# Three edits at the joints of a four-layer graph kernel: filling matmuls, the home of four sums, the order of the last three norms

## The chip, the cores and the metric

The kernel runs on one core of a Trainium2 chip. The metric is the device time of one execution in microseconds; the median of three executions is given.

## What is computed

Four layers over x (8 graphs of 2048 nodes with 64 features, float32) share one dense 2048 x 2048 adjacency matrix A. Each layer adds its result to its input and normalises over the 64 features. Cut to what matters:

```python
# layer 0: Chebyshev graph convolution with a weight per node, w[n] = embedding[n] @ weight
x = ln(x + sum_k (T_k(A) x)[n] @ w[n, k] + b[n])       # T_0 = I, T_1 = A, T_2 = 2 A A - I
# layer 1: two plain steps
z = relu(A x @ W0);  z = relu(A z @ W1);  x = ln(x + z)
# layer 2
x = ln(x + x @ W_self + (A x) @ W_neigh + b2)
# layer 3: diffusion convolution, both supports are A
x = ln(x + [x, Ax, 2AAx - x, Ax, 2AAx - x] @ W3 + b3)

def ln(x): return (x - mean(x)) / sqrt(var(x) + 1e-5)
```

Nearly all the work is products of A with a 2048 x 512 matrix (8 graphs times 64 features).

## The kernel before

x lies in SBUF as `xy`, 128 nodes by 16 node tiles by two slots by 512 columns; a pair p of graphs is 128 columns. A node group i is four node tiles (`TG` = 4). The weights are folded so that the mean over features is zero before a norm, which leaves a norm only squares, a sum, a root and a scaling.

**The first product**, A x of layer 0, goes by four slices of output nodes (L877). Slice 0 is a plain product, `plain_slice` (L767); it takes the slices' matrix chunks in the order `AHEAD` (L162), the first in four parts. Slices 1 to 3 (`fast_slice`, L791) use one level of Winograd's form of Strassen's algorithm, and VectorE meanwhile prepares sums of blocks of A (`prepare`, L622), which GpSimd's queue stores to DRAM as `comb` for the later products. A slice's result is four tiles hT of features by nodes, in the pool tag "t" (5 buffers, L761). Each is stored to DRAM as t1T on SP's queue (L754) and transposed back to nodes (`back`, L763), and so becomes the next product's input. Ahead of all this, TensorE multiplies a tile of zeros with itself eight times while the first data are on their way (L695 to L699).

**The later products** (`product`, L211) use two levels of that algorithm: 7 outer products, each an `inner` (L232) of 7 block products of 8 matmul records per 128 x 512 bank. The outer order is A11, S1, A12, S2, S4, S3, A22. An `inner` needs four sums of its right-hand blocks, t1 to t4 (L242 to L245), which VectorE writes to fresh tiles of tag "t", so they take the buffers that hT or earlier sums give back. The block products come in a fixed order, 0, 5, 1, 6, 4, 3, 7; the second takes t2, the fourth t3. Results are gathered in tiles of tag "C" (4 buffers, L230), each of four blocks: u and v from A11 and S1, and one more for each of two later places. Before the second product, tag "C" holds the block sums of `prepare`.

The order of work on an engine is partly the program's order (`keep_in_program_order`), partly a scheduler's; a pool's tile goes to whichever buffer the scheduler finds free. A `Pump` (L30) runs the layers' smaller jobs one step behind each block product.

**The last product** (`onto_slot=1`, `ends=True`, L1062) has nodes on partitions. Its last `inner` ends in `tail` (L337), which norms its last three blocks: block 3 is added by `finish(3, ...)` (L296) and normed as a job of the pump; block 2 ("1") and block 1 are joined to their partial sums, squared on ScalarE, reduced on VectorE, and so on in an order written out by hand (L355 to L375). The last block product is cut in two halves of two node tiles each (L303, L256), so block 1 has two norms, h0 and h1, of two tiles each. `Norm` (L453) holds the steps: `square`, `add_up`, `variance`, `root` (ScalarE), `refine` (one Newton step, three VectorE instructions), `scale` (VectorE) or `scale_tiles` (ScalarE, one instruction per tile and graph), `store`.

Of the kernel before, what the change touches and what calls it, by code (L numbers as in the profile page):

```python
# [9 lines left out]
F32 = mybir.dt.float32  # L10
# [93 lines left out]
def kernel(  # L104
# [106 lines left out]
    def product(src, feature, between=None, rate=1, own=None, pin=False, runs=None, onto_slot=None, ends=False):  # L211
# [10 lines left out]
        def add(out, a, b, op=ALU.add):  # L222
            nc.vector.tensor_tensor(out, a, b, op)  # L223
            return out

        def new_t():
            return sums.tile([P, NT // 2, 4 * F], F32, tag="T", name="T", bufs=3)

        def new_c():
            return sums.tile([P, 4, GW], F32, tag="C", name="C", bufs=4)  # L230

        def inner(q, b, finish, early=None, tail=None, next_sum=None):  # L232


            b11, b12, b21, b22 = (
                b[:, hm * TG : (hm + 1) * TG, ts(hc, 2 * F)] for hm in range(2) for hc in range(2)
            )

            def new():
                return sums.tile([P, TG, 2 * F], F32, tag="t", name="t", bufs=5)  # L240

            t1 = add(new(), b12, b11, ALU.subtract)  # L242
            t2 = add(new(), b22, t1, ALU.subtract)
            t3 = add(new(), b22, b12, ALU.subtract)
            t4 = add(new(), b21, t2, ALU.subtract)  # L245
            if next_sum is not None:
                next_sum()

            def mul(ps, s, xb, start, stop=True):
                a = load(q, s)  # L250
                if onto_slot is not None:

                    for k in range(TG):
                        for m in range(TG):
                            if isinstance(ps, list):
                                to, opens = ps[k // 2][:, ts(k % 2, P)], k % 2 == 0  # L256
                            else:
                                to, opens = ps[:, ts(k, P)], k == 0
                            nc.tensor.matmul(  # L259
                                to, a[:, k, m, :], xb[:, m, :], start=(start and opens and m == 0),  # L260
                                stop=(m == TG - 1), skip_group_check=True,
                            )
                    pump.step(pump.rate)
                    return
                for m in range(TG):
                    nc.tensor.matmul(  # L266
                        ps, xb[:, m, :], a[:, :, m, :], start=(start and m == 0),
                        stop=(m == TG - 1), skip_group_check=True,
                    )
# [24 lines left out]
            pc = bank("c")  # L294
            mul(pc, 4, t1, True)
            finish(3, pc, u3)  # L296
            if tail is None:
                mul(pb, 3, t4, False)
                finish(2, pb, p1)
                mul(pc, 7, b22, False)  # L300
                finish(1, pc, u2)
            else:
                halves = [p_z.tile([P, GW], F32, tag="z", name=f"mmd{h}") for h in range(2)]  # L303
                tail(pc, pb, halves, lambda: mul(pb, 3, t4, False), lambda: mul(halves, 7, b22, True))
# [29 lines left out]
        def at_the_end(c, ih, ch):  # L334


            def tail(pc, pb, halves, mul2, mul1):  # L337
                pin = tc.keep_in_program_order
                add(c[:, 1], pc, c[:, 1])
                mul2()  # L340
                i = 2 * ih
                n2 = Norm(tiles_of(i + 1), 2 * ch, 1, onto_slot, "1")
                pin(nc.vector.tensor_tensor(n2.flat(), tiled(pb), tiled(c[:, 2]), ALU.add))
                n2.square()
                mul1()
                h = [Norm(slice(i * TG + 2 * k, i * TG + 2 * k + 2), 2 * ch + 1, 1, onto_slot, f"h{k}") for k in range(2)]

                def join(k):
                    half = halves[k][:, : 2 * P].rearrange("p (t c) -> p t c", t=2)
                    pin(nc.vector.tensor_tensor(  # L350
                        h[k].flat(), half, tiled(c[:, 1])[:, 2 * k : 2 * k + 2], ALU.add
                    ))
                    h[k].square()

                n2.add_up()  # L355
                join(0)
                n2.variance()
                n2.root()
                h[0].add_up()
                n2.refine()  # L360
                join(1)
                h[0].variance()
                h[0].root()
                n2.scale_tiles(0, 2)
                h[1].add_up()
                h[1].variance()
                h[0].refine()
                h[1].root()
                n2.scale_tiles(2, 4)
                n2.store(nc.scalar)  # L370
                h[1].refine()
                h[1].scale()
                h[1].store()
                h[0].scale()
                h[0].store()  # L375
            return tail

        def tiled(block):
            return block.rearrange("p (t c) -> p t c", t=TG)
# [7 lines left out]
        def prior(ih, ch):  # L387
# [6 lines left out]

        pump.pass_mark()
        u, v = new_c(), new_c()
        t1 = new_t()
        inner(A11, b11, *fresh(u), next_sum=lambda: tc.keep_in_program_order(
            nc.vector.tensor_tensor(t1, b12, b11, ALU.subtract)
        ))  # L400
        if pump.hold:
# [48 lines left out]
    def tiles_of(i):  # L450
        return slice(i * TG, (i + 1) * TG)

    class Norm:  # L453
# [3 lines left out]
        def __init__(self, tiles, p0, n, slot, tag, pin=True):  # L457
            self.tiles, self.p0, self.n, self.slot, self.tag = tiles, p0, n, slot, tag
            self.pin = tc.keep_in_program_order if pin else lambda inst: inst
            self.nt = tiles.stop - tiles.start  # L460
            self.shape = [P, self.nt, 2 * n, F]
            self.v = self.flat().rearrange("p t (b f) -> p t b f", f=F)

        def flat(self):
# [13 lines left out]
        def square(self, pool=False):  # L478
            if self.n == 1:
                self.sq = sums.tile([P, TG, 2, F], F32, tag="t", name="sq1", bufs=5)[:, : self.nt]  # L480
            else:
                self.sq = small.tile([P, TG, 4, F], F32, tag="sq", name="sq")
            if pool:

                nc.gpsimd.tensor_tensor(self.sq, self.v, self.v, ALU.mult)
            else:
                self.pin(nc.scalar.activation(self.sq, self.v, AF.Square))

        def add_up(self):
            self.ss = self.new("ss")  # L490

            tc.keep_in_program_order(nc.vector.tensor_reduce(self.ss, self.sq, AX.X, ALU.add))

        def variance(self):
            self.pin(nc.vector.tensor_scalar(self.ss, self.ss, 1.0 / F, EPS, ALU.mult, ALU.add))
# [10 lines left out]
            self.pin(nc.vector.scalar_tensor_tensor(nw, nw, -0.5, self.ss, ALU.mult, ALU.mult))  # L506
            self.pin(nc.vector.scalar_tensor_tensor(self.rs, nw, 1.5, self.rs, ALU.add, ALU.mult))

        def scale(self):
            self.pin(nc.vector.tensor_tensor(self.v, self.v, self.wide(self.rs), ALU.mult))  # L510

        def scale_tiles(self, t0, t1):
            for t in range(t0, t1):
# [5 lines left out]
        def store(self, queue=nc.sync):  # L519
            for k in range(self.n):  # L520
                p = self.p0 + k
                queue.dma_start(out[:, p, self.tiles], xy[:, self.tiles, self.slot, ts(p, 2 * F)])

    def layernorm(i, p0, n, slot, mean=False, store=False, pool_sq=False):

# [35 lines left out]
    if True:  # L561
# [127 lines left out]
        with tc.tile_pool(name="p_n", bufs=4, space=PSUM) as p_n, tc.tile_pool(  # L689
# [5 lines left out]
            zero = sums.tile([P, GW], F32, tag="p1", name="zero")[:, :P]  # L695
            nc.vector.memset(zero, 0.0)
            rise = p_tn.tile([P, TG, P], F32, tag="pt", name="rise")
            for k in range(8):
                nc.tensor.matmul(rise[:, k % TG, :], zero, zero, start=True, stop=True)  # L699

            bias0 = small.tile([P, F], F32, tag="bias0", name="bias0")
# [409 lines left out]
```

## Time and profile before

| | |
|---|---|
| runs, not profiled | 1672.47, 1672.82, 1674.05 us (median 1672.82) |
| the profiled execution's own time | 1675.26 us |
| its span, first to last instruction | 1673.5 us |
| TensorE busy | 1661.9 us (99%) |
| VectorE busy | 946.2 us (57%) |
| ScalarE, GpSimd busy | 266.4 us (16%), 246.0 us (15%) |
| mean DMA rate | 234 GB/s |

PE is TensorE's matmuls, PEld its weight loads, DVE VectorE, ACT ScalarE, POOL GpSimd, SP SyncE, which here only issues DMAs. An fp32 matmul shows as two records. In a timeline the columns are the start and the duration in us, the engine with the line, the operation with output <- input, the shapes and the count of merged records; in brackets stands the idle time ahead of it and what ended it. In the list of waits the columns are who waited for whom, the total in us, how often, and the longest. An engine name with a q is its queue, on which it issues DMAs.

### The profile page before, as it was taken

How to read it: one execution, taken by the hardware profiler on the slowest of the kernel's cores; microseconds unless marked ns; L12 is line 12 of the kernel's file. 1: busy time of each engine (PE TensorE's matmuls, PEld its weight loads, DVE VectorE, ACT ScalarE, POOL GpSimd, SP SyncE). 2: the span in 40 equal slices, each digit the busy share in tenths (PEclk: the TensorE clock that was granted, in tenths of full speed). 3: DMA queues.
4: the chain of work that ended last, by engine and by line, in shares of the span. 5: the costliest groups of instructions: out<-in, count | busy, mean ns of one | idle time of the engine just before them, and what ended most of it. 6: DMA issues, size and time to landing. Idle time of an engine off the chain costs nothing.

```text
span 1673.5 us, 20693 instructions
## 1 busy us (share of the span) xinstructions
PE 1661.9 (99%) x8176; PEld 1046.0 (63%) x8176; DVE 946.2 (57%) x1699; ACT 266.4 (16%) x773; POOL 246.0 (15%) x332
## 2 busy tenths in 40 slices
PE   9999999999999999999999999999999999999997
PEld 4688844444444444444454455599998455579997
DVE  5487884456456456654434365873568344453667
ACT  0000000143143044430010011220001011100002
POOL 1121200154055056650000000000000000000000
PEclk9999999999999999999999999999999999999999
DMA  9898898504602700019877877667888866678994
GB/s 348 330 370 311 299 329 304 200 25 138 239 26 101 276 26 26 26 46 365 293 261 273 307 264 253 227 225 262 294 299 298 306 210 235 229 259 299 316 315 151
DMA packets 82432, 391.53 MB, mean 234 GB/s; under 512 B 8896, under 2 KB 25536, under 8 KB 42784
## 3 DMA queue, kind: packets, MB, share of 16 engines
q1 hardware_dynamic: 68992, 346.51, 58.6%
q0 software_dynamic: 11248, 42.08, 6.5%
q10 hardware_dynamic: 2096, 1.61, 0.3%
q8 instruction: 65, 1.06, 0.3%
q14 instruction: 31, 0.25, 0.0%
HBM read 339.85 MB, written 50.33 MB: 233 GB/s over the span
## 4 chain that ended last, share of the span: by engine, by line
PE 98%; DVE 1%; DMA 0%; issue 0%; ACT 0%; DVEq 0%; ACTq 0%
PE y L954 20%; PE mmb L266 17%; PE mma L266 11%; PE mmc L266 11%; PE mmb L259 9%; PE ps_n L813 9%; PE mma L259 6%; PE mmc L259 6%; PE ps_n L776 3%; PE z L1006 3%; PE z L1035 2%; PE pt L997 1%; PE pt_n L447 0%; DMA xy<-in_x 0%; DVE xm L906 0%; DVE xy L910 0%
## 5 line engine op out<-in xcount | busy, mean ns | idle before, releaser
L266 PE MATMUL mmb<-a,t 128*128 128x512 f32 x672 | 302.9, 593 | 0.8 <-DVE t L223 0.8
L964 DVE SCALAR_TENSOR_TENSOR xy<-y,e_sb,xy 128x128 f32<-128x128 f32 x512 | 179.6, 351 | 141.2 <-PE y L954 125.3
L266 PEld LDWEIGHTS mmb<-a,t 128*128 128x128 f32 x672 | 126.0, 190 | 152.2 <-issue 148.8
L973 POOL TENSOR_TENSOR s<-s 128x512 f32<-128x512 f32 (+2 forms) x192 | 157.1, 818 | 335.0 <-ACT s L968 324.8
L968 ACT ACTIVATE s<-y,e_sb 128x128 f32<-128x128 f32 x512 | 138.9, 382 | 231.9 <-PE y L954 220.0
L223 DVE TENSOR_TENSOR u<-mmb,p 128x512 f32<-128x512 f32 x84 | 57.8, 688 | 180.7 <-PE mmb L266 125.2
L259 PE MATMUL mmb<-t,a 128*128 128x128 f32 x1344 | 156.9, 275 | 0.0
L259 PEld LDWEIGHTS mmb<-t,a 128*128 128x128 f32 x1344 | 153.5, 192 | 0.0
L954 PE MATMUL y<-wn,xT 64*128 64x512 f32 x512 | 131.5, 590 | 0.0
L954 PE MATMUL y<-wn,tT 64*128 64x512 f32 x512 | 131.2, 589 | 0.0
L954 PE MATMUL y<-wn,C 64*128 64x512 f32 x512 | 131.2, 589 | 0.0
L266 PE MATMUL mma<-a,T 128*128 128x512 f32 x256 | 115.5, 594 | 0.0
L266 PE MATMUL mmc<-a,t 128*128 128x512 f32 x224 | 100.9, 592 | 0.0
L281 ACT COPY p<-mma 128x512 f32<-128x512 f32 x42 | 24.6, 586 | 405.2 <-PE mma L266 263.4
L954 PEld LDWEIGHTS y<-wn,xT 64*128 64x128 f32 x512 | 49.4, 187 | 61.1 <-issue 60.6
L954 PEld LDWEIGHTS y<-wn,C 64*128 64x128 f32 x512 | 49.6, 187 | 60.3 <-issue 60.3
L954 PEld LDWEIGHTS y<-wn,tT 64*128 64x128 f32 x512 | 49.5, 187 | 60.3 <-issue 60.3
L266 PE MATMUL mma<-a,xy 128*128 128x512 f32 x192 | 86.7, 593 | 0.0
L266 PEld LDWEIGHTS mma<-a,T 128*128 128x128 f32 x256 | 47.6, 190 | 56.8 <-issue 56.5
L223 DVE TENSOR_TENSOR C<-mmc,C 128x512 f32<-128x512 f32 x49 | 33.9, 691 | 85.9 <-PE mmc L266 75.1
L266 PEld LDWEIGHTS mmc<-a,t 128*128 128x128 f32 x224 | 41.6, 190 | 47.4 <-issue 47.1
L813 PE MATMUL ps_n<-a,xy 128*128 128x256 f32 x288 | 64.4, 379 | 0.0
(133 smaller groups left out, 2028.3 us busy)
## 6 DMA issues: line engine op xcount, KB each, us to landing
a<-comb SPq DMA_DIRECT2D x240, 1024.0 KB, 4.8
a<-in_blocks SPq DMA_DIRECT2D x54, 1024.0 KB, 4.8
comb<-si POOLq DMA_DIRECT2D x28, 1024.0 KB, 10.8
a<-in_slices SPq DMA_DIRECT2D x15, 1024.0 KB, 9.1
comb<-so POOLq DMA_DIRECT2D x16, 512.0 KB, 6.3
comb<-so POOLq DMA_DIRECT2D x16, 256.0 KB, 7.9
t1T<-hT SPq DMA_DIRECT2D x16, 256.0 KB, 4.7
xT<-in_xT SPq DMA_DIRECT2D x16, 256.0 KB, 3.3
```

The source lines that it names most:

```text
L223: nc.vector.tensor_tensor(out, a, b, op)
L259: nc.tensor.matmul(to, a[:, k, m, :], xb[:, m, :], start=(start and opens and m == 0), stop=(m == TG - 1), skip_group_check=True,)
L266: nc.tensor.matmul(ps, xb[:, m, :], a[:, :, m, :], start=(start and m == 0), stop=(m == TG - 1), skip_group_check=True,)
L281: nc.scalar.copy(p1, pa)
L776: mm = nc.tensor.matmul(ps[p], xcol(0, TG * j + m, p), ch[j][:, m], start=(n == 0 and m == 0), stop=(n == NG - 1 and m == TG - 1), skip_gr ...
L813: nc.tensor.matmul(ps[:, ts(p, GW // 2)], b(k, p), a(k // TG, k % TG), start=(start and p == k == 0), stop=(k == NT // 2 - 1), skip_group_ ...
L954: mm = nc.tensor.matmul(y[:, b, :], terms[n][half, ts(k, P)], wn[half, n, h * DH : (h + 1) * DH, :], start=(n == 0), stop=(n == 2),)
L964: nc.vector.scalar_tensor_tensor(acc, y[:, :, ts(d, F)], e, acc, ALU.mult, ALU.add)
L968: nc.scalar.activation(s[:, d], y[:, :, ts(d, F)], AF.Copy, scale=e)
L973: nc.gpsimd.tensor_tensor(s[:, :n], s[:, :n], s[:, n : 2 * n], ALU.add)
L1006: nc.tensor.matmul(z[:, k, :], aT[:, ts(k, P)], wd[:, w, :], start=(n == 0), stop=(n == len(terms) - 1),)
L1035: nc.tensor.matmul(z[n][:, k], xT[half, ts(k, P)], w[half], start=True, stop=True)
```

## The change

In front, eleven filling matmuls instead of eight. In the second product (the first call of `product`, the only one with `runs`), the four sums of the first `inner` go to a tile of tag "C", `home`, instead of four tiles of tag "t". In the last product, `tail` writes out the norms of all three last blocks in one order; block 3 is no longer a job of the pump, the last block product is cut in three node tiles and one instead of two and two, block 1 has one norm whose join, square and reduction come in those two parts, block 2's scaling is one tile on ScalarE and three on VectorE, and all stores go through SP.

```diff
-        def inner(q, b, finish, early=None, tail=None, next_sum=None):
+        def inner(q, b, finish, early=None, tail=None, next_sum=None, home=None):
...
+            places = [] if home is None else [tiled(home[:, k]) for k in range(4)]
+
             def new():
+                if places:
+                    return places.pop(0)
                 return sums.tile([P, TG, 2 * F], F32, tag="t", name="t", bufs=5)
...
-                                to, opens = ps[k // 2][:, ts(k % 2, P)], k % 2 == 0
+                                to = ps[k // (TG - 1)][:, ts(k % (TG - 1), P)]
+                                opens = k % (TG - 1) == 0
...
             mul(pc, 4, t1, True)
-            finish(3, pc, u3)
             if tail is None:
+                finish(3, pc, u3)
                 mul(pb, 3, t4, False)
...
-            def tail(pc, pb, halves, mul2, mul1):
+            def tail(pc, pb, parts, mul2, mul1):
                 pin = tc.keep_in_program_order
-                add(c[:, 1], pc, c[:, 1])
+
+                def norm(blk, tag):
+                    return Norm(tiles_of(2 * ih + blk // 2), 2 * ch + blk % 2, 1, onto_slot, tag)
+
+                def join(n, t0, t1, ps, blk):
+                    pin(nc.vector.tensor_tensor(n.flat()[:, t0:t1], ps, tiled(c[:, blk])[:, t0:t1], ALU.add))
+                    n.square(t0=t0, t1=t1)
+
+                n3, n2, n1 = norm(3, "e3"), norm(2, "1"), norm(1, "e1")
+                join(n3, 0, TG, tiled(pc), 3)
+                pin(nc.vector.tensor_tensor(c[:, 1], pc, c[:, 1], ALU.add))
                 mul2()
-                i = 2 * ih
-                n2 = Norm(tiles_of(i + 1), 2 * ch, 1, onto_slot, "1")
-                pin(nc.vector.tensor_tensor(n2.flat(), tiled(pb), tiled(c[:, 2]), ALU.add))
-                n2.square()
+                n3.add_up()
+                n3.variance()
+                n3.root()
+                n3.refine()
+                join(n2, 0, TG, tiled(pb), 2)
                 mul1()
-                h = [Norm(slice(i * TG + 2 * k, i * TG + 2 * k + 2), 2 * ch + 1, 1, onto_slot, f"h{k}") for k in range(2)]
-
-                def join(k):
-                    half = halves[k][:, : 2 * P].rearrange("p (t c) -> p t c", t=2)
-                    pin(nc.vector.tensor_tensor(
-                        h[k].flat(), half, tiled(c[:, 1])[:, 2 * k : 2 * k + 2], ALU.add
-                    ))
-                    h[k].square()
-
+                n3.scale()
+                n3.store()
                 n2.add_up()
-                join(0)
                 n2.variance()
                 n2.root()
-                h[0].add_up()
+                cut = TG - 1
+                join(n1, 0, cut, tiled(parts[0])[:, :cut], 1)
                 n2.refine()
-                join(1)
-                h[0].variance()
-                h[0].root()
-                n2.scale_tiles(0, 2)
-                h[1].add_up()
-                h[1].variance()
-                h[0].refine()
-                h[1].root()
-                n2.scale_tiles(2, 4)
-                n2.store(nc.scalar)
-                h[1].refine()
-                h[1].scale()
-                h[1].store()
-                h[0].scale()
-                h[0].store()
+                join(n1, cut, TG, tiled(parts[1])[:, :1], 1)
+                n1.add_up(0, cut)
+                n1.add_up(cut, TG)
+                n1.variance()
+                n2.scale_tiles(0, 1)
+                n1.root()
+                n2.scale(1, TG)
+                n2.store()
+                n1.refine()
+                n1.scale(0, cut)
+                n1.store(0, cut)
+                n1.scale(cut, TG)
+                n1.store(cut, TG)
             return tail
...
         u, v = new_c(), new_c()
+
+        home = new_c() if runs is not None else None
         t1 = new_t()
-        inner(A11, b11, *fresh(u), next_sum=lambda: tc.keep_in_program_order(
+        inner(A11, b11, *fresh(u), home=home, next_sum=lambda: tc.keep_in_program_order(
...
-        def scale(self):
-            self.pin(nc.vector.tensor_tensor(self.v, self.v, self.wide(self.rs), ALU.mult))
+        def scale(self, t0=0, t1=TG):
+            shape = [P, t1 - t0, 2 * self.n, F]
+            rs = self.rs[:, t0:t1].unsqueeze(3).to_broadcast(shape)
+            self.pin(nc.vector.tensor_tensor(self.v[:, t0:t1], self.v[:, t0:t1], rs, ALU.mult))
...
-            for k in range(8):
+            for k in range(11):
                 nc.tensor.matmul(rise[:, k % TG, :], zero, zero, start=True, stop=True)
```

`square`, `add_up` and `store` take a range of node tiles in the same way as `scale`.

More of the change, by code (lines that the diff above doesn't have):

```diff
@@ L302, in inner @@
             else:
-                halves = [p_z.tile([P, GW], F32, tag="z", name=f"mmd{h}") for h in range(2)]
-                tail(pc, pb, halves, lambda: mul(pb, 3, t4, False), lambda: mul(halves, 7, b22, True))
+                parts = [p_z.tile([P, GW], F32, tag="z", name=f"mmd{h}") for h in range(2)]
+                tail(pc, pb, parts, lambda: mul(pb, 3, t4, False), lambda: mul(parts, 7, b22, True))
         def fresh(c):
@@ L459, in __init__ @@
             self.pin = tc.keep_in_program_order if pin else lambda inst: inst
-            self.nt = tiles.stop - tiles.start
-            self.shape = [P, self.nt, 2 * n, F]
+            self.shape = [P, TG, 2 * n, F]
             self.v = self.flat().rearrange("p t (b f) -> p t b f", f=F)
@@ L476, in center, with square @@
             nc.vector.scalar_tensor_tensor(self.v, self.wide(sm), -1.0 / F, self.v, ALU.mult, ALU.add)
[L478 to L482, printed above, removed]
+        def square(self, pool=False, t0=0, t1=TG):
+            if t0 == 0:
+                if self.n == 1:
+                    self.sq = sums.tile([P, TG, 2, F], F32, tag="t", name="sq1", bufs=5)
+                else:
+                    self.sq = small.tile([P, TG, 4, F], F32, tag="sq", name="sq")
             if pool:
@@ L486, in square, with add_up @@
             else:
[L487 to L492, printed above, removed]
+                self.pin(nc.scalar.activation(self.sq[:, t0:t1], self.v[:, t0:t1], AF.Square))
+        def add_up(self, t0=0, t1=TG):
+            if t0 == 0:
+                self.ss = self.new("ss")
+            tc.keep_in_program_order(
+                nc.vector.tensor_reduce(self.ss[:, t0:t1], self.sq[:, t0:t1], AX.X, ALU.add)
+            )
         def variance(self):
@@ L517, in scale_tiles, with store @@
                     ))
-        def store(self, queue=nc.sync):
+        def store(self, t0=0, t1=TG):
+            tiles = slice(self.tiles.start + t0, self.tiles.start + t1)
             for k in range(self.n):
                 p = self.p0 + k
-                queue.dma_start(out[:, p, self.tiles], xy[:, self.tiles, self.slot, ts(p, 2 * F)])
+                nc.sync.dma_start(out[:, p, tiles], xy[:, tiles, self.slot, ts(p, 2 * F)])
     def layernorm(i, p0, n, slot, mean=False, store=False, pool_sq=False):
```

## The prediction

> **What bounds the kernel now.** I read the page first, then TensorE's waits, then the timeline at the three places that the change touches. All times are from the span's start.
>
> ```profile
> PE 1661.9 (99%) x8176; PEld 1046.0 (63%) x8176; DVE 946.2 (57%) x1699; ACT 266.4 (16%) x773; POOL 246.0 (15%) x332
> ...
> PE 98%; DVE 1%; DMA 0%; issue 0%; ACT 0%; DVEq 0%; ACTq 0%
> ```
>
> TensorE is the bound, and the chain that ended last stays on it. It follows that time can be won only where TensorE stands still or runs slow, and after its last matmul. Its waits in the first 250 us (there are none later):
>
> ```profile
> PE mmb L266 <- DVE t L223: 0.8, 1, 0.8
> PE ps_n L776 <- DMA xy<-in_x: 0.6, 1, 0.6
> PE pt_n L447 <- ACT xy L448: 0.3, 1, 0.3
> PE mmc L266 <- DVE C L223: 0.3, 1, 0.3
> ```
>
> The front, from the timeline of weight loads (the matmuls go with them; an fp32 matmul is two records):
>
> ```profile
> 1.06 3.49 PEld L699 LDWEIGHTS rise<-zero 128*128 128x128 f32 x16 [1.06 <-DVE zero L696]
> 5.45 0.50 PEld L776 LDWEIGHTS ps_n<-a,xy 128*128 128x128 f32 x2 [0.90 <-DMA xy<-in_x]
> 7.43 0.50 PEld L776 LDWEIGHTS ps_n<-a,xy 128*128 128x128 f32 x2 [1.49 <-DMA xy<-in_x]
> 8.45 0.34 PEld L776 LDWEIGHTS ps_n<-a,xy 128*128 128x128 f32 x1 [0.52 <-issue]
> 9.30 0.21 PEld L776 LDWEIGHTS ps_n<-a,xy 128*128 128x128 f32 x1 [0.52 <-issue]
> 9.75 0.19 PEld L776 LDWEIGHTS ps_n<-a,xy 128*128 128x128 f32 x1 [0.24 <-issue]
> ```
>
> Up to 9.3 us the loads come 0.85 us apart, then 0.43: TensorE runs at half clock until then. The trace's clock record has full clock from 9.33 to 1668.20 us.
>
> The second product's first sums, VectorE and TensorE:
>
> ```profile
> 218.71 0.68 DVE L223 TENSOR_TENSOR t<-xy 128x512 f32<-128x512 f32 x1
> 221.36 0.69 DVE L223 TENSOR_TENSOR t<-xy,t 128x512 f32<-128x512 f32 x1 [1.97 <-PE mma L266]
> ...
> 222.11 3.70 PE L266 MATMUL mmb<-a,t 128*128 128x512 f32 x8 [0.81 <-DVE t L223]
> ...
> 239.81 3.70 PE L266 MATMUL mmc<-a,xy 128*128 128x512 f32 x8 [0.27 <-DVE C L223]
> ```
>
> VectorE stands 1.97 us before t2. The named releaser, mma, is not it: the t buffer still holds an hT, and the first store t1T<-hT landed at 221.24, 0.12 us ahead.
>
> The tail:
>
> ```profile
> 1661.34 3.74 PE L259 MATMUL mmd<-T,a 128*128 128x128 f32 x32
> ...
> 1668.40 0.76 DVE L510 TENSOR_TENSOR xy<-xy,rs 128x256 f32<-128x256 f32 x2
> ```
>
> TensorE ends at 1665.08, VectorE at 1669.16; the last store was issued at 1669.33 and landed at 1672.05; then 1.4 us of end work.
>
> **What the Trainium skill says.** "TensorE: Matmul & The Clock Gate", Part 1: The HAM clock gate: the clock starts at half rate and is released after a busy window of 3413 ns that runs free of the kernel. The trace agrees: 1668.20 - 9.33 = 1658.87 us is 486.0 windows of 3.4133, so window edges lay at 2.50, 5.92 and 9.33. The window 2.50 to 5.92 held the pause between filling and first product and did not count as busy; the next did. "VectorE: DVE Perf Modes", The TRN2 errata: fp32 tensor_tensor takes (N+151)/0.96 ns; the trace has 0.69 for 512 and 0.42 for 256, as it says, so I use 0.56 for 384 and 0.29 for 128, forms the trace lacks. "DMA: Bandwidth & Descriptors", Anatomy of one DMA, gives about 2.0 us plus bytes at 436 GB/s (for GpSimd's path). Here a lone 256 KB store took 2.29 us: first packet 0.92 after the issue, data at about 290 GB/s, semaphore 0.4 after. The measurement decides.
>
> **Front: 3 more filling matmuls** (6 records, 0.213 us apart at half clock). Sixteen records went out by 4.42; 22 go to about 5.92. The first product's data are there at 5.45, so it starts up to 0.47 later. The second pair of products waits for its xy piece until 7.43 anyway; two records at half clock from 5.92 end at 7.6 to 7.9, at full clock before 7.43. So the delay costs between 0 and 0.35. In return TensorE is busy without a pause from 1.06. With this run's window edges the clock rises at 5.92. From 7.43 the records go 0.43 apart: the fourth after it starts at 7.43 + 3 x 0.43 = 8.72, where it was 9.75: 1.03 won. The edges run free, so another execution wins (rise - 7.43)/2, with a rise between some 8.4 and 11.3: 0.5 to 1.9. Then who is late next? SP's loads, whose waits for TensorE move with it, but whose data come through full DMA engines:
>
> ```profile
> 79.79 3.62 PE L813 MATMUL ps_n<-a,xy 128*128 128x256 f32 x16
> ...
> 80.90 1.23 DVE L627 TENSOR_TENSOR so<-a 128x1024 f32<-128x1024 f32 x1 [15.96 <-DMA a<-in_slices]
> ```
>
> VectorE waits 16 us for the last chunk of the second slice, which lands at 80.88. TensorE needs it halfway through its row, at 81.5: only 0.64 us to spare. If the landing does not move (DMA share was above 1.0 from 45 to 75 us, 0.59 from 75 to 80), 0.64 is all that passes. I take -0.8, between 0.64 and 1.03; ends +0.35 (zeros don't count as activity; no run here shows it) and -1.6.
>
> **Middle: t1 to t4 of product 1 in a C tile.** Same four additions, another place. In the built order the first of them now waits for a store comb<-si that landed at 197.8 in this trace; no t1T store is waited for. From 218.71, t1, t3 and t2 at 0.60 apart: t2 done at 220.6. TensorE's sixth mma record starts at 220.71, so mmb could start at 221.14; it started at 222.11, and its first record after a pause was 0.10 longer (3.70 against 3.60): 0.97 + 0.10 = 1.07 won. VectorE then runs 2.3 us ahead through the centering, without a pause (223.48 to 239.07 it was busy throughout); the addition C<-mmc, at 239.07 before, comes at about 237.3, and TensorE wants it at 239.38 - 1.07 = 238.3. So the second wait goes too: 239.81 - (235.94 + 8 x 0.43) + 0.10 = 0.53. Sum -1.6. The margin of the second is about 0.3 us after the addition's own 0.68, so its bound is -1.07. A gain cannot be undone by loads: the fifth block of this product is issued at 222.44 behind tT and lands at 229.37, needed at 231.4; later ones are issued as TensorE frees a ring buffer and move with it. What is held instead: a fifth C tile in a pool of four. See the rivals.
>
> **Tail.** The products keep their order and count; the last is split 24 and 8 records instead of 16 and 16, so the first part ends at 1664.18, the second at 1665.08. VectorE after, with the trace's pitches (0.20 between dependent small operations, 0.085 between independent ones, 0.03 from ACT or TensorE to VectorE, 0.095 to ACT): join of the "1" block 1661.53 (was 1661.97, behind a scale), its square 1662.31, reduction 1662.97, reciprocal 1663.89, root 1664.13. Join of three tiles 1664.21, refine to 1665.09, join of the last tile 1665.17; squares 1664.86 and 1665.55, reductions 1665.42 and 1665.89; one variance 1666.21, reciprocal 1666.42, root 1666.66. Three tiles of "1" are scaled on VectorE under that root at 1666.52, refine 1666.99 to 1667.39, scales 1667.59 and 1668.06, end 1668.35: 0.81 ahead of 1669.16. The gain is one statistics chain of 8 columns in place of two of 4, and two scales per tile on ACT in place of eight. SP issues at 1668.18 and, 0.46 later, 1668.64 (was 1669.33): 0.69. And the data: before, 512 KB left together, moving from 1669.7 to 1671.7; after, 256 KB leave at 1667.12 and are done by 1669.0, 192 KB follow from 1669.1 and the last 64 KB end near 1670.0; plus 0.4: 1670.4 against 1672.05. I take -1.6; if the last store keeps its 2.72 us from issue to landing, -0.7; ends -0.7 and -1.8. The block normed first (e3) gets its scale and store 0.8 us later; they have 5 us of cover.
>
> **Sum**: -0.8 - 1.6 - 1.6 = -4.0 us. The profiled execution's 1675.26 (span 1673.5 and 1.8 around it) becomes 1671.3; it lies 2.4 above the median of the unprofiled runs, 1672.82, which becomes 1668.8.
>
> **Rivals.** (1) The front gives nothing: the zeros don't raise the clock, or the chunk at 80.88 takes all back. For it: the thin 0.64; against it: before's own windows. -3.2 + 0 = -3.2: 1669.6. (2) The tail's last store keeps its latency, as the small ones took 2.6 to 2.7 here: -3.1: 1669.7. (3) Slower: the fifth C tile. If the tile of S2 had to wait for one that is still in use, VectorE, and behind it TensorE, would stand for about one inner product of 7 steps of 3.43: 24 us, 1692.8. It decides if the borrowed tile is free later than the first write of S2's tile at 302.64. Against it: the last matmuls that read it end at 239.5, and that write waits only for VectorE in the built order. That the change isn't done is excluded by the same order: only these three places differ.
>
> **Chances.** Forecast 0.64, (1) 0.17, (2) 0.16, (3) 0.03. About 0.2%, 3.35 us, is what a measurement can tell: the line is at 1669.5. The forecast lies below it but for a small part; (1) and (2) lie just above it, a third of each below: faster 0.71, same 0.26, slower 0.03. Range: all at their good ends give 1667.8, less 0.4 for the spread of the runs; above, -2.0 (front 0, second wait kept, tail -0.9): 1670.8.
>
> **What would show it.** Loads 0.43 apart from about 7.4 us on (or a rise still at 8.4 to 11.3: the front is wrong); no wait of TensorE at mmb and mmc near 222 and 239; perhaps a new wait at ps_n L813 near 81; VectorE's end some 3.3 us after TensorE's instead of 4.1, and the last landing 5.3 after it instead of 7.0. A wait of VectorE near 302 would make it all wrong.

## The result

The kernel after the change takes 1670.68 us at the median of 22 runs (1670.23 to 1671.09), the kernel before, on the same chip, 1672.99 us (22 runs, 1672.38 to 1675.1). The ratio is 0.9985, 95% interval [0.9978, 0.9991]: 2.31 us less, or 0.14%. That is less than the forecast's 4.0 us, inside its range near the upper end, and below the 0.2% that the prediction took as the line between faster and no difference. The execution that was profiled took 1670.91 us (span 1669.1), only 0.2 above its median, where that of the kernel before, 1675.26, lay 2.3 above its own.

From the page of the kernel after, engine totals and chain:

```profile
PE 1660.6 (99%) x8182; PEld 1046.5 (63%) x8182; DVE 945.8 (57%) x1695; ACT 265.3 (16%) x766; POOL 246.0 (15%) x332
...
PE 98%; DMA 1%; DVE 0%; ACT 0%; issue 0%; ACTq 0%; DVEq 0%
```

TensorE stays the bound. It has six more records and yet 1.3 us less busy time: full clock comes at 5.41 us, ahead of the first product, and no longer at 9.33, behind its first records. The chain now has 1% of DMA, because it runs through one transfer of 19.03 us for slice 1 (below); that is not 1% lost. TensorE's waits:

```profile
PE rise L715 <- DVE zero L712: 1.1, 1, 1.1
PE pt_n L457 <- ACT xy L458: 0.3, 1, 0.3
PE ps_n L792 <- DMA xy<-in_x: 0.2, 1, 0.2
```

Both waits of the second product, at mmb and mmc, are gone. The front, from the timeline of weight loads:

```profile
1.06 4.59 PEld L715 LDWEIGHTS rise<-zero 128*128 128x128 f32 x22 [1.06 <-DVE zero L712]
5.57 0.30 PEld L792 LDWEIGHTS ps_n<-a,xy 128*128 128x128 f32 x2
6.86 0.30 PEld L792 LDWEIGHTS ps_n<-a,xy 128*128 128x128 f32 x2 [0.98 <-DMA xy<-in_x]
7.39 0.19 PEld L792 LDWEIGHTS ps_n<-a,xy 128*128 128x128 f32 x1 [0.24 <-issue]
```

From 7.39 on, the loads are 0.43 apart, the pitch of full clock; the trace's clock record has it from 5.41. The second pair still waits for its piece of xy. The second product, VectorE and TensorE:

```profile
217.59 1.29 DVE L223 TENSOR_TENSOR C<-xy 128x512 f32<-128x512 f32 x2
...
218.79 1.41 DVE L223 TENSOR_TENSOR C<-xy,C 128x512 f32<-128x512 f32 x2
...
220.02 1.45 PE L272 MATMUL mmb<-a,C 128*128 128x512 f32 x3
```

The four sums follow one another without a pause, and mmb starts as soon as mma's records are through. The tail:

```profile
1658.62 3.74 PE L265 MATMUL mmd<-T,a 128*128 128x128 f32 x32
...
1664.77 0.76 DVE L525 TENSOR_TENSOR xy<-xy,rs 128x384 f32<-128x384 f32 x2
```

VectorE ends at 1665.53, 3.17 us after TensorE's 1662.36 (4.08 before); the last landing is at 1667.66, 5.30 after (6.97 before).

### The profile page after: what moved, and what is told of

Its sections match the earlier page's. It is cut to its first block, busy times and chain, and to the rows that moved or that the text cites. A ratio compares the mean times of both kernels' runs of the same rounds, so it can differ in the third digit from the quotient of the medians.

```text
span 1669.1 us, 20686 instructions
## 1 busy us (share of the span) xinstructions
PE 1660.6 (99%) x8182; PEld 1046.5 (63%) x8182; DVE 945.8 (57%) x1695; ACT 265.3 (16%) x766; POOL 246.0 (15%) x332
## 4 chain that ended last, share of the span: by engine, by line
PE 98%; DMA 1%; DVE 0%; ACT 0%; issue 0%; ACTq 0%; DVEq 0%
PE y L970 20%; PE mmb L272 17%; PE mma L272 12%; PE mmc L272 12%; PE mmb L265 9%; PE ps_n L829 8%; PE mma L265 6%; PE mmc L265 6%; PE ps_n L792 3%; PE z L1022 3%; PE z L1051 2%; DMA a<-in_slices 1%; PE pt L1013 1%; DMA xy<-in_x 0%; PE pt_n L457 0%; PE mmd L265 0%
## 5 line engine op out<-in xcount | busy, mean ns | idle before, releaser
L272 PE MATMUL mmb<-a,t 128*128 128x512 f32 x648 | 292.0, 593 | 0.0
L272 PEld LDWEIGHTS mmb<-a,t 128*128 128x128 f32 x648 | 121.5, 190 | 145.3 <-issue 143.5
L272 PE MATMUL mmc<-a,t 128*128 128x512 f32 x216 | 97.3, 592 | 0.0
```

Source lines behind the costliest of these rows:

```text
L272: nc.tensor.matmul(ps, xb[:, m, :], a[:, :, m, :], start=(start and m == 0), stop=(m == TG - 1), skip_group_check=True,)
```

## The experiments

All times below are compared with runs of the kernel before that were made on the same chip beside them (medians 1672.94, 1672.93 and 1672.89). Such a ratio has an interval of about 0.08% either way, 1.3 us, so that the parts are read from the traces first. This table has, for each trace, the stretch from the span's start to the ninth record of the first product, slice 1 (from its first record to the start of its first product with sums of A), the second product from its first mma record to the second mmc, and the tail from the start of the last matmul record to the last landing, all in us. A record is one of the two parts as which an fp32 matmul shows, a store lands when its completion is signalled, and "full clock from" is where the trace's clock record goes from half to full, the rise:

| trace | full clock from | ninth record | slice 1 | second product | tail |
|---|---|---|---|---|---|
| before, as shown | 9.33 | 11.04 | 24.60 | 22.54 | 7.25 |
| before_again | 7.18 | 9.67 | 24.60 | 22.04 | 7.25 |
| front_only (11 fillings) | 4.15 | 9.39 | 24.61 | 22.40 | 7.24 |
| middle_only (home tile) | 4.08 | 9.48 | 24.60 | 21.04 | 7.24 |
| tail_only (new tail) | 5.54 | 9.41 | 24.97 | 22.34 | 5.58 |
| fill4 (4 fillings) | 8.27 | 10.32 | 24.61 | 21.71 | 7.24 |
| after | 5.41 | 9.54 | 24.99 | 21.04 | 5.58 |
| after_fill8 (8 fillings) | 6.30 | 9.80 | 24.60 | 21.04 | 5.59 |

The first four runs took the change apart. Each expectation sets two theories, A and B, against each other; they are named anew in each run, so that A of one run is not A of the next.

**before_again**, the kernel before, unchanged, profiled once more.

> The kernel before, unchanged, for a second trace. Its first profiled execution, 1675.26 us, lies 2.3 above the median 1672.99 of its other runs, and the change moved that median by 2.3 where the two traces differ by 4.4. Theory A (that execution was a slow one because the clock rose late in front): an execution near 1673.0, whose front rows are some 1 to 2 us ahead of the first trace's, while the waits at mmb and mmc in the second product (0.8 and 0.3) and the tail (7.0 us from TensorE's end to the last landing) are the same. Theory B (the loss lay in the second product or in the tail): those waits or that tail are shorter by some 2 us in this trace, the front equal.

Measured: 1673.38 us, span 1671.6, 1.9 less than in the first profile. Weight loads, and then waits:

```profile
6.62 0.66 PEld L776 LDWEIGHTS ps_n<-a,xy 128*128 128x128 f32 x2 [1.00 <-DMA xy<-in_x]
7.52 0.19 PEld L776 LDWEIGHTS ps_n<-a,xy 128*128 128x128 f32 x1 [0.24 <-issue]
7.95 0.19 PEld L776 LDWEIGHTS ps_n<-a,xy 128*128 128x128 f32 x1 [0.24 <-issue]
```

```profile
PE mmb L266 <- DVE t L223: 0.3, 1, 0.3
...
PE mmc L266 <- DVE C L223: 0.3, 1, 0.3
```

With eight fillings the loads are 0.43 apart from 7.52 on, as in the kernel after. The front is ahead of the first trace's and the tail is the same, as theory A said. But A also had the wait at mmb the same, and that is wrong: it is 0.3 where the first profile had 0.8. Of the 1.88 us between the two traces of one and the same kernel, the front has 1.37 and the second product 0.50.

**front_only**, before with the extra fillings alone:

```diff
-            for k in range(8):
+            for k in range(11):
```

> Before with eleven filling matmuls, nothing else. Theory A: most executions of before already have their clock early, or are held by the chunk that lands near 80.9 us; the median moves by -0.5 to 0.1 us, and the slowest runs (1674 to 1675) vanish. Theory B, by the prediction's own term: -0.8 to -1.1 us in the median.

Measured: 1673.25 us (13 runs, 1672.87 to 1673.69), ratio 1.0002 [0.9994, 1.001]. The prediction's -0.8 is not there at the median; A's -0.5 to 0.1 lies within the interval. The 13 runs spread over 0.8 us, where the kernel before has 2.2 over the 33 runs beside them, but that this is the fillings' doing is not shown: middle_only, with eight, spreads over 0.6. In the lists of runs, 1 of 108 with eleven fillings lies more than 1 us above the median of its list, and 11 of 220 with eight. This points the way of theory A, which had the slowest runs vanish, and is too little to show it.

**middle_only**, before with the four sums in the tile of tag "C":

```diff
+            places = [] if home is None else [tiled(home[:, k]) for k in range(4)]
...
+        home = new_c() if runs is not None else None
```

> Before with the four first sums of the second product in a C tile, nothing else. Theory A: -1.0 to -1.6 us in the median, the two waits of TensorE gone. Theory B: -0.2 to -0.8, since the waits of the one trace were longer than usual.

Measured: 1672.17 us (1671.83 to 1672.4), ratio 0.9996 [0.9988, 1.0004]: -0.77, which is what theory B of this run said. In its trace both waits are gone and the second product takes 21.04 us.

**tail_only**, the kernel after with eight fillings and without the home tile:

```diff
-            for k in range(11):
+            for k in range(8):
...
-        home = new_c() if runs is not None else None
+        home = None
```

> Before with the new order of the last three norms and the cut of three and one node tiles, nothing else. Theory A: -1.3 to -1.7 us in the median, 5.3 us from TensorE's end to the last landing. Theory B: -0.5 to -1.0.

Measured: 1671.38 us (1670.92 to 1672.2), ratio 0.9991 [0.9983, 0.9999]: -1.56. The tail takes 5.58 us, 1.67 less than in the kernel before: what the prediction's -1.6 and theory A said. The three parts alone give +0.3, -0.8 and -1.6, together -2.0; the whole change gave -2.3.

The next four asked what the fillings do and what makes the tail shorter.

**fill4**, before with four fillings (`range(4)` in the line above).

> The kernel before with four filling matmuls instead of eight. Theory A (eight already give an early rise in most executions; a window counts if TensorE is busy in about four fifths of it, and TensorE then waits for its xy piece in any case): with four the filling ends near 2.7 us and TensorE pauses until about 4.9, so that no window that holds the pause counts. The clock rises between 7.6 and 11.0 us wherever the window edges lie, the products from 6.6 us on go 0.85 apart until then: +0.3 to +2.0, at the middle +1.1 us against the kernel before, about 1674.0. Theory B (the filling counts for little, the half clock hides behind the data): 0, within 0.3 us, in spite of a late rise.

Measured: 1675.10 us (1673.73 to 1676.34), ratio 1.0012 [1.0004, 1.002], +2.2 us with an interval from 0.7 to 3.3. Its weight loads:

```profile
1.06 1.78 PEld L699 LDWEIGHTS rise<-zero 128*128 128x128 f32 x8 [1.06 <-DVE zero L696]
5.23 0.50 PEld L776 LDWEIGHTS ps_n<-a,xy 128*128 128x128 f32 x2 [2.39 <-DMA xy<-in_x]
7.05 0.50 PEld L776 LDWEIGHTS ps_n<-a,xy 128*128 128x128 f32 x2 [1.32 <-DMA xy<-in_x]
8.07 0.29 PEld L776 LDWEIGHTS ps_n<-a,xy 128*128 128x128 f32 x1 [0.52 <-issue]
8.60 0.19 PEld L776 LDWEIGHTS ps_n<-a,xy 128*128 128x128 f32 x1 [0.24 <-issue]
```

The loads pause 2.39 us ahead of the first product (the matmuls 2.1), and full clock comes at 8.27, after the data. So the fillings do count, and the half clock is not hidden: theory B falls. That zeros raise the clock is seen most directly in the table: middle_only has full clock at 4.08 and front_only at 4.15, ahead of their first data at 5.16 and 5.32. The measured +2.2 is twice the middle of what A expected, though A's value lies in the interval. The execution that was profiled, 1673.73 us, is the fastest of the 13 and has a front 0.65 us behind that of before_again; where the other 1.4 us of the median lie was not seen.

**after_fill8**, the kernel after with eight fillings again.

> The kernel after with eight filling matmuls again, home tile and tail as changed. Theory A (the three extra fills give nothing at the median): -2.3 us against the kernel before, as the kernel after, rise of the clock at 3.6 to 7.0 us in a typical trace, middle and tail as in the kernel after. Theory B (the front's -0.8 is real but hidden in the spread): -1.5 us.

Measured: 1670.57 us (21 runs, 1670.34 to 1672.52), ratio 0.9987 [0.998, 0.9993]: -2.36, as theory A said. The whole gain is there without the extra fillings. The ratio's interval, -3.3 to -1.2 us, would leave room for theory B; but tail_late_n2 (below), which repeats the kernel after with eleven fillings, took 1670.53 us on the same chip at the same time, a difference of 0.04. Two of the 21 runs, 1672.11 and 1672.52, lie apart, as single ones of the kernel before do. That these had a late rise is not shown: they were not profiled.

**tail_late_n2** and **late_n2_pinned**, the kernel after with block 2's store issued last:

```diff
                 n2.scale(1, TG)
-                n2.store()
...
                 n1.store(cut, TG)
+                n2.store()
```

> The kernel after with the 256 KB store of block 2 issued after both stores of block 1, so that all 512 KB leave within one microsecond; VectorE's order is kept. If the early leave of these 256 KB is what the stores' half of the tail's gain consists of (0.76 us), the last landing comes 0.8 to 1.0 us later after VectorE's end than in the kernel after (2.12 us there), at 2.9 to 3.1, and VectorE's end stays 3.46 us after the start of the last matmul. If the stores are not limited by what is under way (each lands 2.3 us after its own issue), the last one, issued some 0.9 us later, lands 0.95 us later as well, but the two of block 1 then land 2.0 to 2.1 us after their issues as before; if they share the DMA engines they land later than that.

Measured: 1670.53 us (1670.07 to 1670.9), and the last landing 2.14 after VectorE's end. But the edit had moved nothing: the store is not tied to the program's order, and the scheduler put it where it had been. The instructions stand in the order of the kernel after on every engine, so this is a second trace of that kernel (second product 21.04, tail 5.59) and tells nothing of the stores. In late_n2_pinned `store` is kept in program order as well:

```diff
-                nc.sync.dma_start(out[:, p, tiles], xy[:, tiles, self.slot, ts(p, 2 * F)])
+                self.pin(nc.sync.dma_start(out[:, p, tiles], xy[:, tiles, self.slot, ts(p, 2 * F)]))
```

> The kernel after with the store of block 2 issued last on SP's queue, this time pinned there (the scheduler had put tail_late_n2 back into the order of the kernel after, so that run was a repeat of it). VectorE's order is kept. If the stores' half of the tail's gain (0.76 us from VectorE's end to the last landing) comes from block 2's 256 KB leaving ahead of the others, the last landing comes 2.9 to 3.1 us after VectorE's end (2.12 in the kernel after). If what counts is only how late the last issue is and how small that store is, a lone 256 KB store issued 0.46 us behind the last one of the kernel after and needing 2.3 us ends 2.8 to 2.9 us after VectorE's end, and the stores of block 1 land 1.8 to 2.1 us after their issues as before.

Measured: 1671.62 us (1671.24 to 1671.95), ratio 0.999 [0.9982, 0.9999]. VectorE ends 3.44 us after the start of the last matmul, as in the kernel after (3.46), and the last landing comes 3.17 after that instead of 2.12: 1.05 us for the place of one store, and a little more than either theory said. DMA issues of the tail (KB of each, median us from issue to landing), late_n2_pinned first, then the kernel after:

```profile
out<-xy SPq DMA_DIRECT2D x2, 256.0 KB, 2.3
out<-xy SPq DMA_DIRECT2D x1, 192.0 KB, 2.1
out<-xy SPq DMA_DIRECT2D x1, 64.0 KB, 1.9
```

```profile
out<-xy SPq DMA_DIRECT2D x2, 256.0 KB, 2.3
out<-xy SPq DMA_DIRECT2D x1, 192.0 KB, 2.1
out<-xy SPq DMA_DIRECT2D x1, 64.0 KB, 1.8
```

Each store takes what it took, so with issues 0.5 us apart they hardly hinder one another. The last one is issued 0.53 later after VectorE's end (0.82 against 0.29) and is a 256 KB store, which takes 2.34 instead of 1.84: together the 1.05, within 0.02. This prices the place of a large store; it does not show what slowed the stores of the kernel before (see tail_cut2).

**tail_cut2**, the kernel after with the last block product cut in two and two tiles:

```diff
-                                to = ps[k // (TG - 1)][:, ts(k % (TG - 1), P)]
-                                opens = k % (TG - 1) == 0
+                                to = ps[k // 2][:, ts(k % 2, P)]
+                                opens = k % 2 == 0
...
-                cut = TG - 1
+                cut = TG - 2
...
-                join(n1, cut, TG, tiled(parts[1])[:, :1], 1)
+                join(n1, cut, TG, tiled(parts[1])[:, :2], 1)
```

> The kernel after with the last block product cut in two and two node tiles instead of three and one; the new order is kept. If the small last part is what shortens the chain behind the last matmul: join 0.42 instead of 0.29, square and reduction each some 0.1 longer, so VectorE's end 0.3 to 0.4 us later than in the kernel after. If the order and the single set of statistics are what brings the gain, VectorE's end is the same within 0.1 us and the last store, now 128 KB instead of 64, lands up to 0.2 us later.

Measured: 1670.87 us (1670.44 to 1671.18), ratio 0.9988 [0.9981, 0.9994]. VectorE ends 3.77 us after the start of the last matmul (3.46 in the kernel after), the last landing 5.82 (5.58). From its timeline of VectorE:

```profile
1662.37 0.42 DVE L350 TENSOR_TENSOR xy<-mmd,C 128x256 f32<-128x256 f32 x1 [0.16 <-PE mmd L265]
1662.71 0.41 DVE L504 TENSOR_REDUCE ss<-sq 128x4 f32<-128x256 f32 x1
1663.28 0.42 DVE L504 TENSOR_REDUCE ss<-sq 128x4 f32<-128x256 f32 x1 [0.16 <-ACT sq L497]
```

VectorE now waits for ScalarE's square of the second part. The 3/1 cut is worth 0.3 us at VectorE's end, 0.24 at the landing; the rest of the tail's 1.67 is the order, the one set of statistics and the stores. Of the stores this run shows more. Block 1 goes out in two stores of 128 KB, as in the kernel before and as far apart (0.46 us). Their DMA issues and block 2's in the kernel before, then block 1's here:

```profile
out<-xy ACTq DMA_DIRECT2D x1, 256.0 KB, 2.9
out<-xy SPq DMA_DIRECT2D x2, 128.0 KB, 2.7
```

```profile
out<-xy SPq DMA_DIRECT2D x2, 128.0 KB, 1.9
```

In the kernel before, block 2's 256 KB were issued 0.14 us ahead of them, on ScalarE's queue; here 0.90 ahead, on SP's. The two stores take 1.89 us each, where they took 2.62 and 2.72. So stores of the same size land 0.7 to 0.8 us sooner once block 2's store leaves well ahead of them. Whether its earlier issue or its other queue does it was not separated.

**act_scale**, the kernel after with the last tile scaled on ScalarE, beside VectorE, and stored through ScalarE's queue (`store` takes the queue):

```diff
-                n1.scale(cut, TG)
-                n1.store(cut, TG)
+                n1.scale_tiles(cut, TG)
+                n1.store(cut, TG, nc.scalar)
```

> The kernel after with the last node tile of block 1 scaled by two instructions on ScalarE beside VectorE's scaling of the other three, and stored through ScalarE's queue, so that neither the second scale on VectorE (0.28 us) nor the second issue on SP (0.46 us behind the first) stands on the path. If the end is a chain of instructions and issues, VectorE ends 0.48 us earlier, both stores leave within 0.15 us of each other and the last landing is 0.2 to 0.45 us earlier: 5.15 to 5.4 us after the start of the last matmul (5.58 in the kernel after); about -0.3 us, less than the times can show. If the landing of the 192 KB store is what ends last, 0.1 or nothing: 5.4 to 5.6.

Measured: 1670.79 us (21 runs, 1670.22 to 1675.24), ratio 0.9988 [0.9981, 0.9994], no better than the kernel after. VectorE ends 0.21 earlier, not 0.48: the first scale's own end had stood only 0.20 ahead. Both stores are issued 0.09 apart, and the last landing comes 5.69 us after the start of the last matmul, 0.11 later than in the kernel after.

```profile
out<-xy SPq DMA_DIRECT2D x1, 192.0 KB, 2.4
out<-xy ACTq DMA_DIRECT2D x1, 64.0 KB, 2.1
```

Issued together they take 2.4 and 2.1 us instead of 2.1 and 1.8, and here the 192 KB store lands last, 0.17 after the small one. So what was won ahead of the small store is lost on the large one: scaled and stored in this way, a quicker last tile is worth nothing.

**home1**, middle_only with only t1 in the tile of tag "C", by the list of places:

```diff
-            places = [] if home is None else [tiled(home[:, k]) for k in range(4)]
+            places = [] if home is None else [tiled(home[:, k]) for k in range(1)]
```

> The kernel before with only the first of the four sums, t1, in a tile of tag C; t2 then takes the fifth t buffer and t3 is the one that waits for the landing of the first store of t1T. If the prediction's reading of the first wait is right, TensorE's wait at mmb (0.3 to 0.8 us in five traces) is gone, 0.7 to 1.0 us of the middle's gain is there by the second product's first block products, and the rest (the wait at mmc, 0.2 to 0.3) stays, since VectorE still loses the time ahead of its centering: from the start of mma to the start of the second mmc 21.2 to 21.5 us, where the kernel with the full tile needs 21.04 and the kernel before 21.7 to 22.5. If something else held t2 (TensorE's mma, as the trace names it), the wait at mmb stays.

Measured: 1672.30 us (1671.76 to 1673.0), ratio 0.9996 [0.9988, 1.0005]: -0.59. From VectorE's timeline:

```profile
218.06 0.68 DVE L223 TENSOR_TENSOR C<-xy 128x512 f32<-128x512 f32 x1
218.78 0.69 DVE L223 TENSOR_TENSOR t<-xy,C 128x512 f32<-128x512 f32 x1
219.67 0.69 DVE L223 TENSOR_TENSOR t<-xy 128x512 f32<-128x512 f32 x1 [0.20 <-DMA t1T<-hT]
```

The third sum is now the one that waits, and the trace names the store t1T<-hT as what it waits for. That is what the prediction had argued for the second sum against the name in the trace. The second product takes 21.04 us, as with the full tile; that the wait at mmc would stay was wrong. In this trace the store landed 3.0 us after the first mma record (3.1 to 4.0 in the five traces with all sums in tag "t"), so VectorE lost only 0.20. Whether one tile is enough where the store lands late was not seen.

## Why the prediction was right and where it failed

The parts, in us:

| part | predicted | against the trace it was priced from | its run alone, median |
|---|---|---|---|
| front | -0.8 | -1.50, of which slice 1 gave back 0.39 | +0.3 |
| middle | -1.6 | -1.50 | -0.8 |
| tail | -1.6 | -1.67 | -1.6 |
| whole | -4.0 | -4.35 | -2.3 (the change itself) |

**Against the trace it was made from, the sum holds.** From 1675.26 to 1670.91 are 4.35 us, and the prediction took 4.0 off. The stretches of the table make 4.28 of it.

**The step that failed is the last one: "it lies 2.4 above the median of the unprofiled runs", and the sum was taken from that median unchanged.** This treats the 2.4 us as a constant that both kernels carry. It was the stalls themselves: that execution had a late rise of the clock and a long wait at mmb, and of its excess over the second trace of the same kernel these two have all (1.37 and 0.50 of 1.88). A median execution had less to lose, and the change cannot take from it what it does not have. That the median still lies in the range is in part luck: the range's slow end, -2.0, stood for no gain in front, the wait at mmc kept and a tail of -0.9. What came is nearly as small by another path: no gain in front, both waits gone but worth half, and the full tail.

**Front: predicted -0.8, measured 0 at the median** (front_only +0.3 within its interval; after_fill8 and tail_late_n2 0.04 apart). The traces agree: the ninth record comes at 9.39 to 9.90 us in the six with eleven fillings and at 9.40 to 9.80 in five of the six with eight; only the one of the prediction has 11.04. The mechanism was right, as fill4 shows, but the term was priced with one execution's window edges, that is, the times at which one busy window ends and the next begins. The prediction's "another execution wins (rise - 7.43)/2, with a rise between some 8.4 and 11.3" is wrong: of six other traces with fewer than eleven fillings, only fill4's rises after 7.2. In the traces here a window counts although TensorE stands for part of it. With eight fillings at half clock the last of the 16 records starts at 4.42 and, at their pitch of 0.21, is through at 4.64 us; the first product starts when its data are there, 5.02 to 5.45 us. Windows, counted back from the rise in steps of 3.41 us, with up to 0.65 us of pause were followed by full clock (before_again, 3.77 to 7.18); those with 0.70 or more were not (before, 2.50 to 5.92, with 0.81). Of the executions with eight fillings only the one whose first data came latest, at 5.45, fell through. And a rise before 7 us wins next to nothing over another one: the second pair of products waits for its piece of xy until 6.6 to 7.4 in any case. The prediction saw that wait and used it only to price the delay. "TensorE: Matmul & The Clock Gate", Part 1: The HAM clock gate, which the prediction cited for the free windows, says in the same place that the number of matmuls at half clock differs from run to run with the phase and should not be fitted to one count. This is what the term did; the traces agree with the page, with rises from 4.08 to 9.33 us.

**The chunk of slice 1.** The prediction gave the front's gain a cap, as a landing at 80.88 leaves 0.64 us. In the kernel after TensorE did wait there:

```profile
78.29 4.00 PE L829 MATMUL ps_n<-a,xy 128*128 128x256 f32 x16
```

4.00 us where the row needs 3.62: 0.38 lost. The chunk's landing moves by itself, though: tail_only lost 0.37 and home1 0.8 with eight fillings, front_only nothing with eleven. From issue to landing the chunk took 17.5 to 18.3 us in the ten traces without a loss, and 19.0, 19.0 and 19.4 in after, tail_only and home1. It is no answer to the front's gain in particular.

**Middle: predicted -1.6, measured -1.5 in the trace it was priced from, about -0.8 at the median.** What waits for what was right (home1, and no wait in any of the traces with a home tile, always 21.04 us). It had to be argued against the name in the first trace; the other four traces with the sums in tag "t" name the store themselves, as before_again does for t2:

```profile
219.47 0.69 DVE L223 TENSOR_TENSOR t<-xy,t 128x512 f32<-128x512 f32 x1 [1.45 <-DMA t1T<-hT]
```

The size of the wait is the landing of that store: t2 started 0.12 to 0.13 us after it in all five, and mmb 0.75 after that, from 4.01 to 4.84 us after the first mma record. The prediction's trace had the longest. The mean of the five is 1.17 us over 21.04, a little above what the times give (-0.77 middle_only, -0.59 home1, and -0.8 between tail_only and after_fill8); these agree within their intervals, and the difference is not settled.

**Tail: predicted -1.6, measured -1.67 in the traces and -1.56 in the times.** Both halves came as worked out: VectorE's end -0.91 (predicted -0.81), the landing another -0.76 (predicted -0.84). The first comes from the chain of instructions, 0.3 of it from the cut; the second from block 2's store leaving ahead of block 1's, as tail_cut2 shows: two stores of the same size as before, 0.7 to 0.8 us quicker, with queue and time of issue not separated. Put last instead, block 2's store costs 1.05 (late_n2_pinned). "VectorE: DVE Perf Modes", The TRN2 errata, gave the prediction 0.56 and 0.29 us as estimates for the two forms that the trace lacked; the timeline has 0.56 for two of the three instructions of 384 elements (0.51 for the third) and 0.28 for 128. The tail is the same from execution to execution: 7.24 or 7.25 us in six traces with the old one, 5.58 or 5.59 in four with the new.

**Rivals.** The first (the front gives nothing) is what happened at the median, by neither of the ways it named: the zeros do raise the clock. Its 1669.6 is still 1.1 too low, 0.8 of it the middle's term. The second (the last store keeps its latency) is out: 1.84 us from issue to landing, where it was 2.72. The third (a fifth C tile makes VectorE wait near 302) is out: VectorE's first write of S2's tile, at 299.92 us, follows the instruction ahead of it as it did in the kernel before, and TensorE's list of waits has none that could come from it.

## What to carry to other kernels

A stall that ends with a free-running clock window or with the landing of a transfer has a size that differs from execution to execution; take it from several profiles of the unchanged kernel, or from what the spread of its times allows. If the profiled execution stands above the median, its excess can be made of just the stalls that the profile shows, as it was here, so a sum of removed stalls must not be carried over to the median unchanged. The chain of instructions behind the last matmul and its last stores, in contrast, took the same time in every trace here, and was priced from one trace to a tenth of a microsecond.

## What the runs showed of the hardware

- Matmuls on zeros raise the clock: in middle_only and front_only full clock came at 4.08 and 4.15 us, when TensorE had multiplied nothing else.
- A clock window need not be busy throughout: with 0.62 to 0.65 us of pause in 3.41 it still brought full clock (tail_only, home1, before_again), with 0.70 to 0.86 it did not (before_again, before, tail_cut2). With the records counted at their pitch, this gives an estimate of near four fifths busy for the bound; the profile's own, modelled ends of the records would put it higher, and the bound itself was not measured.
- Stores that leave together slow one another. Two of 192 and 64 KB issued 0.09 us apart on two queues took 2.4 and 2.1 us to land; 0.47 us apart on one queue 2.1 and 1.8. Two of 128 KB took 2.62 and 2.72 us behind a store of 256 KB issued 0.14 us ahead on another queue, and 1.89 each where it was issued 0.90 ahead on the same one. Time and queue changed together in both.
- The landing of one and the same transfer moves between executions: the first t1T store ahead of the second product is issued 1.63 us before the first mma record in all thirteen traces and lands 2.95 to 4.16 us after it; in the two traces of the unchanged kernel, 3.98 and 3.45.
